# Places copied by GpSimd, scatters handed over together, an early base for the sums and separate weight loads in a routed expert layer

## The chip, the core and the metric

The kernel runs on one core of one Trainium2 chip. The metric is device time in microseconds of one execution; less is better. Instructions are issued in order on each engine: TensorE (PE, with its weight loads PEld), VectorE (DVE), ScalarE (ACT), GpSimd (POOL), and SyncE (SP), which here issues nearly all plain transfers. GpSimd issues the indirect ones.

## The reference

32 sequences of 256 tokens with 128 features: 8192 tokens. A modulation is computed for each sequence, then a gated linear recurrence along the tokens, then a mixture of 8 experts of which each token takes the best two.

```python
mod = (silu(c) @ wmod).reshape(32, 6, 1, -1)          # sa, ca, ga, sb, cb, gb
h = layernorm(x) * (1 + ca) + sa
g, a, v = sigmoid(h @ Wg.T + bg), sigmoid(h @ Wd.T + bd), h @ Wv.T + bv
x = x + ga * (scan(h_t = a_t * h_(t-1) + (1 - a_t) * v_t) * g)
h = layernorm(x) * (1 + cb) + sb
probs = softmax(h @ gate_w.T + gate_b)                # 8 experts, the top 2 are kept
y_e = relu(h @ w1[e] + b1[e]) @ w2[e] + b2[e]
x = x + gb * sum over the top 2 of probs_e * y_e
```

Before this, ga and gb are held at an absolute value of at least 0.25, with their sign.

## The kernel before

The 8192 tokens are cut into 16 supertiles of 512 tokens (s = 0 to 15; ST = 512, T = 4 groups of 128). Each goes through four steps, one step behind the other: a_norm (layer norm), a_mix (the recurrence), a_res (adding it to x, second layer norm) and a_route. HEAD and the loop over `steps` write the order of these steps by hand.

a_route picks two experts for each token, counts how many rows each expert has had so far (the product pq, L439 and L441, and the sum rk, L449), and so gets for each of the 2 x 512 rows a place in the DRAM array `reg`, in which each expert's rows lie together. The rows (`rw`: 128 features, the gate, the row's own number) are scattered to their places by eight indirect transfers of 128 rows each (L473), with the places read from the tile `pi`. They aren't issued at once: `sending` keeps them, and `drip` hands over one or two per step, each behind an ACT instruction that it names (`a["last"]`, `b["last"]`).

After some supertiles (TAKE, and the last one) `table` finds which full blocks of 256 rows the experts now have. There are 71 blocks. They enter `blocks` when drip has handed over the last scatter of that supertile (`held`). b_step moves a pipeline of blocks on by one:

- b_load: SP reads the block's expert and first row from the table (L561, L562), then loads the rows `xr` (L564, after the last sixteen reg scatters) and the expert's up weights `ww` (L570), four blocks ahead (LOOK).
- b_in: TensorE transposes the rows (L577) into `pbx`; ACT and DVE split them into two parts `xs` (L579, L580).
- b_up: twelve products (L592 to L594) into `p1`; ACT and DVE apply bias and relu (L598, L600).
- b_down: sixteen products (L611) into the one buffer `pby`; ACT scales by the gate into `yt` (L615, eight buffers); two indirect transfers (L617) scatter the 256 rows to the DRAM array `yd`, with the places read from `xr`.

`between` calls b_step between the steps of the supertiles while enough blocks wait. What is left runs alone at the end. When all blocks that hold rows of a supertile have gone through b_down, c_load loads its rows from yd (`yk`, L634) and transposes its gates (`pg`, L626, DVE L628), and c_add sums: yk's two halves (L648), the bias product pz (L644, added in L649), times the modulation gt (L642, L652), plus x (L653), and the result goes out (L654). The last supertile's sum waits for the last block.

The build runs with a scheduler: it takes each engine's order from its own simulation and the priorities in `high_priority`, so the order of the text is not the order of the queues.

## Time and profile before

| What | Value |
| --- | --- |
| Three runs, median (lowest to highest) | 541.54 us (541.11 to 545.75) |
| The profiled execution, its time | 542.55 us |
| The profiled execution, its span | 540.9 us |
| Mean granted TensorE clock | 0.861 |
| Moved by DMA | 91.57 MB, 169 GB/s over the span |
| Scatters to reg (L473) and to yd (L617) | 128 and 142 |
| GpSimd's time for one of them | 0.98 and 0.995 us |

The span reaches from the first to the last instruction. Busy shares are averages over stages with different limits: up to about 108 us the first supertiles are prepared and weights are staged, up to 342 us supertiles are routed with blocks between, then blocks run, and from 456 us blocks and sums. A line of the waits names the engine that waited, the line, and what came last before it went on; "issue" is time in which it waited for nothing that the profile shows. Landing is when a transfer's semaphore says that its data are there.

### The profile page before, as it was taken

To read this page: it belongs to the slowest core of one execution; us is meant where nothing else is said; L and a number is where in the kernel's file an instruction comes from. 1 tells how busy PE (TensorE), PEld (TensorE's weight loads), DVE (VectorE), ACT (ScalarE), POOL (GpSimd) and SP (SyncE) were. 2 spreads that over 40 slices of the span, in tenths; PEclk is the share of its full clock that TensorE was granted. 3 is DMA by queue.
4 is the path that set the end of the run, shared out by engine and by line. 5 is a ranking of instruction groups with operands and counts; after the bars stand their busy time and mean duration, and the time that the engine had idled before them with its cause. 6 is when DMAs were issued, how large, how long until landed. Compare 5 with 4: busy or idle time off the path is not lost. (4 is left out here: it accounts for less than half of the span.)

```text
span 540.9 us, 11312 instructions
## 1 busy us (share of the span) xinstructions
PE 419.9 (78%) x2771; PEld 361.6 (67%) x2771; DVE 305.4 (56%) x1607; ACT 288.2 (53%) x726; POOL 291.7 (54%) x322
## 2 busy tenths in 40 slices
PE   4668667696797878978698678778767999899971
PEld 3234424485676867758587577777666999899870
DVE  7999889583685756557367552412111220666565
ACT  4858355664757557467474453434243556566620
POOL 4535654445555666666565656556665355355531
PEclk9965666797879868997989897898989999899976
DMA  7993110754263534444351564457616887999853
GB/s 225 364 288 140 41 40 22 216 183 118 68 187 98 169 105 136 133 141 135 106 160 52 147 188 140 124 176 201 181 42 194 266 236 218 313 332 324 270 179 116
DMA packets 55414, 91.57 MB, mean 169 GB/s; under 512 B 8655, under 2 KB 39965, under 8 KB 55351
## 3 DMA queue, kind: packets, MB, share of 16 engines
q1 hardware_dynamic: 46624, 73.89, 45.6%
q0 software_dynamic: 8672, 16.94, 9.2%
q8 instruction: 25, 0.41, 0.3%
q14 instruction: 39, 0.31, 0.2%
q10 hardware_dynamic: 54, 0.02, 0.0%
HBM read 64.30 MB, written 27.43 MB: 170 GB/s over the span
## 5 line engine op out<-in xcount | busy, mean ns | idle before, releaser
L617 POOL DMA_INDIRECT yd<-yt,xr x142 | 141.3, 995 | 113.2 <-ACT yt L615 79.4
L611 PE MATMUL pby<-wr,hh 128*128 x1136 | 161.4, 298 | 26.5 <-ACT yt L615 21.3
L473 POOL DMA_INDIRECT reg<-rw,pi x128 | 125.5, 980 | 98.6 <-issue 43.5
L611 PEld LDWEIGHTS pby<-wr,hh 128*128 128x128 f32 x1136 | 152.1, 212 | 37.0 <-ACT yt L615 25.6
L600 ACT ACTIVATE hh<-p,ww 128x256 f32<-128x256 f32 x231 | 95.5, 481 | 46.0 <-remote 13.8
L615 ACT ACTIVATE yt<-pby,xr 128x128 f32<-128x128 f32 x142 | 44.6, 365 | 107.4 <-PE pby L611 30.5
L592 PE MATMUL p<-xs,ww 128*128 128x256 f32 x284 | 90.9, 321 | 12.9 <-DVE hh L598 6.3
L593 PE MATMUL p<-xs,ww 128*128 128x256 f32 x284 | 85.3, 300 | 0.1
L594 PE MATMUL p<-xs,ww 128*128 128x256 f32 x284 | 84.4, 297 | 0.5 <-issue 0.5
L580 DVE TENSOR_TENSOR xs<-pbx,xs 128x256 fp32r<-128x256 f32 x71 | 29.9, 420 | 83.6 <-ACT xs L579 38.1
L362 PE MATMUL pz<-h,wT 128*128 128x512 f32 x96 | 60.1, 750 | 11.0 <-DVE ta L374 7.4
L592 PEld LDWEIGHTS p<-xs,ww 128*128 128x128 f32 x284 | 57.7, 204 | 16.1 <-DVE hh L598 7.8
L594 PEld LDWEIGHTS p<-xs,ww 128*128 128x128 f32 x284 | 58.1, 204 | 1.1 <-issue 1.1
L593 PEld LDWEIGHTS p<-xs,ww 128*128 128x128 f32 x284 | 58.3, 205 | 0.7 <-issue 0.5
L598 DVE TENSOR_SCALAR hh<-p,ww 128x256 f32<-128x256 f32 x53 | 25.4, 479 | 28.8 <-ACT hh L600 20.8
L362 PEld LDWEIGHTS pz<-h,wT 128*128 128x128 f32 x96 | 20.8, 246 | 27.9 <-issue 17.1
L579 ACT ACTIVATE xs<-pbx 128x256 fp32r<-128x256 f32 x71 | 27.4, 386 | 14.1 <-PE pbx L577 6.6
L577 PE MATMUL pbx<-ident,xr 128*128 128x128 f32 x142 | 29.7, 289 | 5.2 <-DMA xr<-reg 2.8
L340 ACT ACTIVATE xn<-xa,nra,nya 128x128 f32<-128x128 f32 x64 | 26.5, 493 | 11.4 <-DVE nra L323 11.4
L398 ACT ACTIVATE xm<-xa,nrb,nyb 128x128 f32<-128x128 f32 x64 | 26.3, 485 | 9.6 <-DVE nrb L323 5.9
L648 DVE TENSOR_TENSOR ot<-yk 128x512 f32<-128x512 f32 (+1 forms) x17 | 11.2, 659 | 29.2 <-DMA yk<-yd 14.3
L577 PEld LDWEIGHTS pbx<-ident,xr 128*128 128x128 f32 x142 | 18.6, 150 | 7.5 <-issue 3.5
(188 smaller groups left out, 614.4 us busy)
## 6 DMA issues: line engine op xcount, KB each, us to landing
ww<-wd SPq DMA_DIRECT2D x71, 514.0 KB
xr<-reg SPq DMA_DIRECT2D x71, 130.0 KB
yk<-yd SPq DMA_DIRECT2D x30, 256.0 KB
wd<-wh SPq DMA_DIRECT2D x8, 514.0 KB
xa<-in_L_attn_x_dram SPq DMA_DIRECT2D x16, 256.0 KB
out_dram<-ot SPq DMA_DIRECT2D x15, 256.0 KB
yd<-yt,xr POOLq DMA_INDIRECT x142
w1s<-in_L_ffn_w_dram SPq DMA_DIRECT2D x8, 256.0 KB
```

Source lines behind the costliest of these rows:

```text
L362: nc.tensor.matmul(z, wT[:, i], h1, start=True, stop=True)
L473: w = nc.gpsimd.indirect_dma_start(out=reg, out_offset=bass.IndirectOffsetOnAxis(ap=pi[:, j * K + k:j * K + k + 1], axis=0), in_=rw[:, j, ...
L577: nc.tensor.transpose(px[:, j * P:(j + 1) * P], xr[:, j, 0:D], ident)
L579: nc.scalar.activation(xs[:, 0], px, AF.Copy)
L580: nc.vector.tensor_tensor(xs[:, 1], px, xs[:, 0], op=ALU.subtract)
L592: nc.tensor.matmul(z, hi, xs[:, 0], start=True, stop=False)
L593: nc.tensor.matmul(z, hi, xs[:, 1], start=False, stop=False)
L594: nc.tensor.matmul(z, lo, xs[:, 0], start=False, stop=True)
L600: w = nc.scalar.activation(hh[:, k], p1[:, k - k0], AF.Relu, bias=bias)
L611: nc.tensor.matmul(py[:, j * D:(j + 1) * D], hh[:, k, j * P:(j + 1) * P], we[:, k * D:(k + 1) * D], start=(j == 0 and k == 0), stop=(j == ...
L615: nc.scalar.activation(yt[:, j], py[:, j * D:(j + 1) * D], AF.Copy, scale=xr[:, j, D:D + 1])
L617: w = nc.gpsimd.indirect_dma_start(out=yd, out_offset=bass.IndirectOffsetOnAxis(ap=xr[:, j, D + 1:D + 2].bitcast(I32), axis=0), in_=yt[:, ...
```

## The change

- `place` copies the 128 places of one scatter into a small tile of its own (eight buffers in rotation), on GpSimd, in front of each scatter to reg and to yd. The scatter reads the copy.
- drip, sending and their waits are taken out. a_route issues its eight scatters itself. A table's blocks enter `blocks` at the next supertile's route step (those of the last table at once). Each block remembers how many scatters had been issued when its table was made, and its rows wait for the sixteen before that.
- b_load is parted: b_weights (four blocks ahead, LOOKW) and b_rows (three ahead, LOOKR), in this order in each step.
- c_base is new: from step CB0 = 28 on, and as soon as a supertile is counted, it computes the bias product, multiplies it by the modulation and adds it to x in place. c_add then sums yk's halves, multiplies and adds x. The modulation is spread twice, once for each (`spread`, `scaled`).
- From block 53 (HA) odd blocks take `pbx` and `pby` from the buffers that the routing used.
- yk has three buffers instead of two, ot three, which the constant b2f now shares; dgT has two instead of four.

```diff
...
+LOOKW = 4
+LOOKR = 3
 HA = 53
+CB0 = 28
...
     def late_constants():
-        b2f = cp.tile([P, T, D], F32, name="b2f")
+        b2f = wk.tile([P, T, D], F32, tag="ot", name="b2f", bufs=3)
         nc.gpsimd.memset(b2f, 0.0)
...
     nc.vector.tensor_copy(pad[:, :, D + 1].bitcast(I32), padi)
+    def place(column, name):
+        t = bk.tile([P, 1], I32, tag="place", name=name, bufs=8)
+        nc.gpsimd.tensor_copy(t, column)
+        return t
...
             w = nc.gpsimd.indirect_dma_start(
-                out=reg, out_offset=bass.IndirectOffsetOnAxis(ap=pi[:, j * K + k:j * K + k + 1], axis=0),
+                out=reg, out_offset=bass.IndirectOffsetOnAxis(ap=place(pi[:, j * K + k:j * K + k + 1], f"pp{s}_{j}{k}"), axis=0),
                 in_=rw[:, j, k], in_offset=None)
             into_reg(w.ins, "scat")
             return w.ins
-        sending.extend((s, send, j, k) for j in range(T) for k in range(K))
+        sent.extend(send(j, k) for j in range(T) for k in range(K))
         return rk[:, T]
-    sending = []
     sent = []
     held = []
-    def drip(n, behind):
-        for _ in range(min(n, len(sending))):
-            s, send, j, k = sending.pop(0)
-            w = send(j, k)
-            tc.add_manual_dep(w, behind.ins.name, WAIT, reason="pace of the rows on their way out")
-            sent.append(w)
-            if not sending or sending[0][0] != s:
-                while held and held[0][0] <= s:
-                    blocks.extend(held.pop(0)[1])
...
-    def b_load(n, tb, i):
+    def b_weights(n, tb, i):
         with tc.issue_after(loaded[-1].ins) if loaded else nullcontext():
             e = nc.sync.value_load(tb[i:i + 1, 0:1], min_val=0, max_val=E - 1)
+        ww = bk.tile([P, WW], F32, tag="ww", name=f"ww{n}", bufs=5)
+        loaded.append(nc.sync.dma_start(ww, wd[bass.ds(e, 1)].rearrange("o p f -> p (o f)")))
+        return dict(n=n, ww=ww, tb=tb, i=i)
+    def b_rows(b):
+        n, tb, i = b["n"], b["tb"], b["i"]
+        with tc.issue_after(loaded[-1].ins):
             r = nc.sync.value_load(tb[i:i + 1, 1:2], min_val=0, max_val=E * CAP)
         xr = bk.tile([P, NJ, RW], F32, tag="xr", name=f"xr{n}", bufs=YTB + 6)
         w = nc.sync.dma_start(xr, reg[bass.ds(r, BLK)].rearrange("(p t) d -> p t d", p=P))
         tc.add_to_no_dep_group("rows", w.ins)
-        for x in sent[-2 * K * T:]:
+        for x in b["sent"]:
             tc.add_manual_dep(w.ins, x.name, WAIT, reason="its rows")
-        ww = bk.tile([P, WW], F32, tag="ww", name=f"ww{n}", bufs=5)
-        b = dict(n=n, xr=xr, ww=ww, tb=tb, i=i)
-        loaded.append(nc.sync.dma_start(ww, wd[bass.ds(e, 1)].rearrange("o p f -> p (o f)")))
-        return b
+        loaded.append(w)
+        b["xr"] = xr
+    def own(n, tag, other):
+        if n >= HA and n % 2:
+            return psa.tile([P, 512], F32, tag=other, name=f"{tag}{n}")
+        return psb.tile([P, 512], F32, tag=tag, name=f"{tag}{n}")
     def b_in(b):
         n, xr = b["n"], b["xr"]
-        px = psb.tile([P, 512], F32, tag="pbx", name=f"pbx{n}")[:, :BLK]
+        px = own(n, "pbx", "pq")[:, :BLK]
         for j in range(NJ):
...
         n, xr, hh, i = b["n"], b["xr"], b["hh"], b["i"]
-        py = psb.tile([P, 512], F32, tag="pby", name=f"pby{n}")[:, :NJ * D]
+        py = own(n, "pby", "pt")[:, :NJ * D]
         e = nc.tensor.value_load(b["tb"][i:i + 1, 0:1], min_val=0, max_val=E - 1)
...
             w = nc.gpsimd.indirect_dma_start(
-                out=yd, out_offset=bass.IndirectOffsetOnAxis(ap=xr[:, j, D + 1:D + 2].bitcast(I32), axis=0),
+                out=yd, out_offset=bass.IndirectOffsetOnAxis(ap=place(xr[:, j, D + 1:D + 2].bitcast(I32), f"pd{n}_{j}"), axis=0),
                 in_=yt[:, j], in_offset=None, bounds_check=K * N - 1, oob_is_err=False)
             for g in ("yscat", "yrows"):
                 tc.declare_no_dep(w.ins, group=g, reason="rows of other pairs")
             tc.add_to_no_dep_group("yscat", w.ins)
+    def c_base(s):
+        pg = psa.tile([P, 512], F32, tag="pq", name=f"pg{s}")[:, :P + BPS * D]
+        nc.tensor.transpose(pg[:, :P], dgx[:, s].rearrange("p h t e -> p (h t e)").bitcast(F32), ident)
+        dgT = wk.tile([P, P], F32R, tag="dgT", name=f"dgT{s}")
+        nc.vector.tensor_copy(dgT, pg[:, :P])
+        g = spread(s, "pt")
+        pz = psa.tile([P, 512], F32, tag="pz", name=f"pb2{s}", bufs=2)
+        nc.tensor.matmul(pz, dgT, b2x.rearrange("p t d -> p (t d)"), start=True, stop=True)
+        t = wk.tile([P, T, D], F32, tag="ot", name=f"tb2{s}", bufs=3)
+        nc.scalar.activation(t.rearrange("p t d -> p (t d)"), pz, AF.Copy)
+        scaled(t, g, range(BPS))
+        nc.vector.tensor_tensor(xa[:, s], xa[:, s], t, op=ALU.add)
+    def spread(s, tag, bufs=1):
+        g = psa.tile([P, 512], F32, tag=tag, name=f"gt{tag}{s}", bufs=bufs)[:, :BPS * D].rearrange("p (q d) -> p q d", d=D)
+        for q in range(BPS):
+            b = s * BPS + q
+            nc.tensor.matmul(g[:, q], sel[:, b:b + 1].to_broadcast([N3, P]), mr3, start=True, stop=True)
+        return g
+    def scaled(t, g, qs):
+        for q in qs:
+            jq = slice(q * JB, (q + 1) * JB)
+            nc.vector.tensor_tensor(t[:, jq], t[:, jq], g[:, q].unsqueeze(1).to_broadcast([P, JB, D]), op=ALU.mult)
     def c_load(s):
-        pg = psa.tile([P, 512], F32, tag="pt", name=f"pg{s}")[:, :P]
-        nc.tensor.transpose(pg, dgx[:, s].rearrange("p h t e -> p (h t e)").bitcast(F32), ident)
-        dgT = wk.tile([P, P], F32R, tag="dgT", name=f"dgT{s}", bufs=4)
-        nc.vector.tensor_copy(dgT, pg)
-        yk = wk.tile([P, K, T, D], F32, tag="yk", name=f"yk{s}")
+        yk = wk.tile([P, K, T, D], F32, tag="yk", name=f"yk{s}", bufs=3)
         step = JB if s >= HALF else T
         for j0 in range(0, T, step):
             for k in range(K):
                 r = k * N + s * ST + j0 * P
                 w = nc.sync.dma_start(tiles(yk[:, k, j0:j0 + step]), tokens(yd, r, step * P))
                 tc.add_to_no_dep_group("yrows", w.ins)
-        return s, yk, step, dgT
-    def c_add(s, yk, step, dgT):
-        gt = psa.tile([P, 512], F32, tag="pq", name=f"gt{s}")[:, :BPS * D].rearrange("p (q d) -> p q d", d=D)
-        for q in range(BPS):
-            b = s * BPS + q
-            nc.tensor.matmul(gt[:, q], sel[:, b:b + 1].to_broadcast([N3, P]), mr3, start=True, stop=True)
-        pz = psa.tile([P, 512], F32, tag="pz", name=f"pb2{s}", bufs=2).rearrange("p (t d) -> p t d", d=D)
-        nc.tensor.matmul(pz, dgT, b2x, start=True, stop=True)
-        ot = wk.tile([P, T, D], F32, tag="ot", name=f"ot{s}")
+        return s, yk, step
+    def c_add(s, yk, step):
+        g = spread(s, "pz", 2)
+        ot = wk.tile([P, T, D], F32, tag="ot", name=f"ot{s}", bufs=3)
         for j0 in range(0, T, step):
             js = slice(j0, j0 + step)
             nc.vector.tensor_tensor(ot[:, js], yk[:, 0, js], yk[:, 1, js], op=ALU.add)
-            nc.vector.tensor_tensor(ot[:, js], ot[:, js], pz[:, js], op=ALU.add)
-            for q in range(j0 // JB, (j0 + step) // JB):
-                jq = slice(q * JB, (q + 1) * JB)
-                nc.vector.tensor_tensor(ot[:, jq], ot[:, jq], gt[:, q].unsqueeze(1).to_broadcast([P, JB, D]), op=ALU.mult)
+            scaled(ot, g, range(j0 // JB, (j0 + step) // JB))
             nc.vector.tensor_tensor(ot[:, js], ot[:, js], xa[:, s, js], op=ALU.add)
...
     nload = 0
-    LOOK = 4
+    based = 0
+    counted = []
+    nrows = 0
     def b_step():
-        nonlocal nload
+        nonlocal nload, nrows
+        nonlocal based
         i = len(flow)
-        while nload < len(blocks) and nload < i + 1 + LOOK:
-            tb, q, ends = blocks[nload]
-            blocks[nload] = b_load(nload, tb, q)
-            blocks[nload]["ends"] = ends
+        while nload < len(blocks) and nload < i + 1 + LOOKW:
+            tb, q, ends, n = blocks[nload]
+            blocks[nload] = b_weights(nload, tb, q)
+            blocks[nload].update(ends=ends, sent=sent[n - 2 * K * T:n])
             nload += 1
+        while nrows < nload and nrows < i + 1 + LOOKR:
+            b_rows(blocks[nrows])
+            nrows += 1
         b = blocks[i] if i < len(blocks) else None
         flow.append(b)
         if b:
             b_in(b)
         if i >= 1 and flow[i - 1]:
             b_up(flow[i - 1])
-            drip(1 if alive else 2, flow[i - 1]["last"])
         if i >= 2 and flow[i - 2]:
             b_down(flow[i - 2])
             ended.extend(flow[i - 2]["ends"])
+        if i >= CB0 and based < min(NS, len(counted)):
+            c_base(based)
+            based += 1
         if len(adding) >= CLAG or (adding and not ended and i >= len(blocks)):
...
                 base = a_route(st[s], base)
+                counted.append(s)
                 if s in CLS:
                     b = cp.tile([P, E], F32, name=f"cnt{s}")
                     nc.vector.tensor_copy(b, base)
                     base = b
                     counts.append(b)
-                nb = len(blocks) + sum(len(x) for _, x in held)
+                while held:
+                    blocks.extend(held.pop(0))
+                nb = len(blocks)
                 if s in TAKE:
                     n = full(s) - nb
                     tb, done = table(s, counts[:1] * (s > CUT) + [base], done, n, False)
-                    held.append((s, [(tb, q, []) for q in range(n)]))
+                    held.append([(tb, q, [], len(sent)) for q in range(n)])
                 elif s == NS - 1:
                     n = touched(s) - nb
                     tb, done = table(NS, counts, done, n, True)
                     fills(base)
-                    rest = [(tb, q, []) for q in range(n)]
-                    held.append((s, rest))
+                    rest = [(tb, q, [], len(sent)) for q in range(n)]
+                    blocks.extend(rest)
                     z = 0
...
             (step0, step1, step2, step3)[i](s)
-            drip(2 if t < len(steps) - NS or len(sending) > K * T else 1, st[s]["last"])
             between()
...
```

1 line of the change is left out of this document (removed).

## The prediction

> **What bounds the kernel now.** I read the page first, then the busy time by stage, then the same view for the down products of line 611 alone. These run sixteen to a block, so their count tells how many of the 71 blocks a stage finishes.
>
> The whole-page shares:
>
> ```profile
> PE 419.9 (78%) x2771; PEld 361.6 (67%) x2771; DVE 305.4 (56%) x1607; ACT 288.2 (53%) x726; POOL 291.7 (54%) x322
> PEclk9965666797879868997989897898989999899976
> DMA  7993110754263534444351564457616887999853
> ```
>
> TensorE is the busiest at 78%, but it is not full in every stage. The next three lines are line 611 alone, in three stages; the columns are the stretch in us, its length, PE busy and count, weight loads busy and count, clock, DMA share and GB/s.
>
> ```profile
> 108.00:337.50 229.50, 72.29 (x480) 68.01 (x481) 0.88 0.45 133
> 337.50:418.00 80.50, 34.57 (x240) 32.47 (x240) 0.90 0.52 151
> 418.00:456.00 38.00, 20.22 (x160) 18.94 (x160) 1.00 0.83 249
> ```
>
> 480, 240 and 160 matmuls are 30, 15 and 10 blocks: 7.65, 5.37 and 3.80 us for each. The first stage still routes supertiles. In the second no supertile is left to route (the last pq product of L439 runs at 341.9 us), yet the pace is far from what TensorE can do. What it can do stands in the chain of waits, where the down products start 3.43 to 3.45 us apart with nothing between but other matmuls:
>
> ```profile
> 440.42 1.78 PE pby L611 x16
> 443.87 1.79 PE pby L611 x16
> 447.30 1.86 PE pby L611 x16
> ```
>
> So the stretch from 337.5 to 418 is the slow zone: 15 blocks at 5.37 us where 3.43 would do. What fills it is GpSimd's queue. There the scatters of the last three supertiles are still handed over one or two per step, each behind an ACT instruction. The waits, in us, times and longest:
>
> ```profile
> POOL yd L617 <- ACT yt L615: 79.4, 46, 5.1
> POOL reg L473 <- ACT hh L600: 19.0, 9, 4.1
> POOL reg L473 <- ACT xm L398: 12.3, 6, 5.6
> SPq L564 <- DMA reg<-rw,pi: 60.6, 18, 11.6
> ```
>
> The last reg scatter starts at 406.5 us, 64.6 us after the last pq, and SP, which may not load the rows of the last table before it has landed, issues no load from 386.3 to 408.9. From 418 TensorE is full; from 456 the sums of the output join, at a DMA share of 0.92.
>
> **The change, part by part.** The sum is made against the profiled execution: 542.55 us, a span of 540.9 and 1.65 around it; the median of the three times, 541.54, lies 1.0 below it.
>
> *Handing over at once (the pace and its waits go).* In the order in which the changed kernel is built, the last pq on TensorE stands behind the down product of block 37; before it stands behind that of block 30. The last reg scatter on GpSimd stands behind the yd scatters of block 33, before behind those of 40. So eight blocks (30 to 37) move from the slow zone under the routing, and the 17 from 38 to 54 can run at the full pace. Before, the 25 blocks 30 to 54 take 456 - 337.5 = 118.5 us. After, 17 x 3.43 = 58.3 us, and the eight cost what they add to the routing stage. Bounds: 3.43 each (packed into TensorE's gaps: by the busy time by stage 229.5 us hold 185.2 of work) is 27 us, 7.65 each (that stage's own pace, routing included) is 61 us. I take 5.37, the pace they have now beside reg scatters: 43 us. Result so far: 118.5 - 58.3 - 43 = 17 us less (bounds 33 less, 1 more).
>
> *The bases.* All sixteen c_base stand before block 38's down product. TensorE: pg 0.27 (L626), pb 0.48 (L644), two gt of 0.225 (L642), 1.2 us x 16 = 19 us if all is on the path, 0 if it fits in the 44 us of gaps. DVE gets two products of 0.415 (L652) and a sum of 0.69 (L653) for each, 24 us, ACT a 512-wide copy (0.69, as L366), 11 us; DVE is busy 135 of 229.5 us there and hides them. If that cover were gone, 1.5 us a supertile would show. I take 6 us more.
>
> *The copies of places.* 270 copies join GpSimd's queue, 196 scatters of which come before the end of the reg scatters (128 and 68). A COPY of 128x4 takes 0.184 us (L264). One that stands between two scatters is seen here:
>
> ```profile
> 251.42 0.98 POOL L617 DMA_INDIRECT yd<-yt,xr  x1 [0.30 <-issue]
> 252.70 0.97 POOL L473 DMA_INDIRECT reg<-rw,pi  x1 [0.30 <-issue]
> 253.66 0.38 POOL L462 COPY rw<-dst 128x8 int32<-128x8 int32 x1
> 254.20 0.98 POOL L473 DMA_INDIRECT reg<-rw,pi  x1 [0.16 <-issue]
> ```
>
> The copy fills the 0.30 us between two scatters, so a pitch of 1.28 becomes 1.50. Bounds for one copy: 0.08 (the median 0.225 of L462 in that gap) and 0.385 (0.225 and a 0.16 gap of its own); I take 0.15, x 196 = 29 us. There are eight buffers, so each copy waits until the scatter eight back has landed, and the rest of the queue waits behind it: the scatters of the yt tiles, and through these ACT and TensorE once eight yt are full. By the built order, up to the end of the reg scatters 5 copies stand directly behind the scatter that they wait for and 25 with one scatter between; the rest have two or more. Landing, from issue, bounded by the two ends that the chain shows:
>
> ```profile
> 451.87 4.29 DMA yd<-yt,xr
> 529.67 2.23 DMA yd<-yt,xr
> ```
>
> Directly behind: 2.23 to 4.29 less one pitch of 1.28, x 5 = 5 to 15 us; one between: 0 to 1.73, x 25 = 0 to 43. I take 20 us, nearer the low end since the first of these two had four scatters in a row behind it. Against that the ACT waits of L473 go: 19.0 + 12.3 + 4.9 + 4.7 + 4.2 + 2.1 = 47 us. Net for GpSimd 29 + 20 - 47 = 2 us; since the eight now stand in one lump before yd scatters, I put 3 us on the path. After the reg scatters 14 copies stand directly behind and 15 one behind their scatter, in pairs. A pair then takes 1.28 + 2.23 + 0.22 + 0.16 = 3.9 us at least where the blocks come every 3.43, 0.5 x 14 = 7 us, which the eight yt buffers (8 x 3.43 = 27 us) cover; were they gone, 7 us would show, at 4.29 us 35.
>
> A rule speaks against the copies. The Trainium skill, SBUF — State Buffer, section Who interferes with whom, says that a GpSimd instruction that reads SBUF is blocked for the whole of a DVE instruction with two SBUF inputs. The trace has GpSimd copies from 0.198 to 0.414 us (L462), so 0.22 us of delay at most; by the rule a copy behind an L653 would lose 0.69 us, and 196 of them at worst 135 us, by the row at worst 43. I go by the row.
>
> *Weights apart.* A ww load no longer stands behind SP's wait for reg (60.6 us in 18 waits). Block 45's up product starts 9.3 us after its loads are issued, the blocks before have 5 to 10 us in hand, so only that one place gains: it is in the 17 us already. 0 more; if a weight came late, each block would show SP's two or three issues of 0.33 us. Rows are asked for three blocks ahead instead of four, 3 x 3.43 = 10 us, where 5 to 10 are needed; the third yk and ot buffers and the shared buffer of b2f cost no instruction.
>
> *The tail from 456.* Leaving it: pg and pb from TensorE (0.12 + 0.24 us apart as issued, 0.36 x 13 = 4.7 us), one DVE sum of 0.69 (L649) of each of the sums. TensorE now waits for DVE ahead of pb (us, times):
>
> ```profile
>   DVE ot L649: 13.8, 11
> ```
>
> With 6.8 ahead of gt that is 20.6 us. This wait stays in part: gt moves to pz's two buffers and still waits for the product of the sum two back, which needs that sum's yk. The second pby and pbx for odd blocks from 53 help only where TensorE isn't already full. The DMA share of 0.92 leaves 0.08 x 57 = 4.6 us in this stage and more after 513. I take 6 us less (bounds 0 and 15).
>
> *Sum.* 542.55 - 17 + 6 + 3 - 6 = 528.5 profiled, 527.5 against the median; I say 527. The bounds add up to 497 and 566, the two outer rivals.
>
> **The rivals.** *GpSimd's queue becomes the bound (slower).* Place: 108 to 418 us, reg scatters, copies and yd scatters in one queue. There it holds 196 x 1.28 = 251 us of 310, so 59 are free. At the high ends the copies add 75 and the waits 58 us, less the 47 of removed pace: 86 us, 27 over what is free; it decides from 59 us on. Lumps of eight also hold up yd, which I price by the longest single wait of SP for reg, 11.6. Together 39 us: 527 + 39 = 566, and from 14 us over the 59, slower than now. For it: queue already 81% taken. Against it: the built order leaves two or more scatters between for 166 of the 196 copies.
>
> *The gain is given back (within 1%).* The eight blocks cost 7.65 each (61 us, 1 more instead of 17 less) and DMA bounds the tail: 541.5 + 1 + 6 + 3 - 6 = 545.5, or 539.5 if the bases fit in the gaps. For it: the routing stage has that pace today.
>
> *All is packed.* Eight blocks at 3.43, bases hidden, tail 15: 541.5 - 33 - 15 + 3 = 497. Against it: no routing stage so far has run TensorE above 81%.
>
> *The change doesn't do it:* if the first reg scatters of each supertile still waited for ACT through the rw buffers (three), the slow zone would stay; that is 541.
>
> **How the numbers follow.** Forecast 0.5 (its own range 515 to 536), packed 0.12, given back or without effect 0.14, GpSimd bound 0.24. About 1%, 5.4 us, is what a measurement can tell from no change. Faster: 0.5 and 0.12, 0.62 in all; within 1%: 0.12; slower: 0.26, which is the GpSimd case and a bit of the second. The range goes to 503 below (half way into the packed case) and 556 above (most of the GpSimd case).
>
> **What would show it.** Right: line 611 counts 38 blocks by about 390 us, then 3.43 to 3.6 us a block until the first sum; no reg scatter after that; SP's wait for reg much below 60.6 us. Wrong: GpSimd near 90% busy with COPY waiting for DMA, yt waiting for yd; line 611 above 4 us a block after the last pq; the last down product later than now (524.6 us).

## The result, and the profile after

The changed kernel takes 607.75 us (median of four, 605.51 to 611.65), the kernel before 542.75 (four, 541.11 to 545.75): ratio 1.122, 95% interval 1.116 to 1.128. It was forecast faster, at 527 us, and is slower by 65. The profiled execution has a span of 604.9 us.

From the page, two lines that answer to those shown of before. GpSimd (POOL) is busy for 48.8 us more, which is less than the time lost, and no engine is near full:

```profile
PE 432.2 (71%) x2803; PEld 365.4 (60%) x2803; DVE 321.4 (53%) x1638; ACT 300.8 (50%) x742; POOL 340.5 (56%) x592
DMA  8972250225443524535354250414557771399983
```

The DMA row dips to 1 near the end (`771399`), where the last ten slices of before hold nothing under 3. Line 621 (before: 611) alone, the down products, sixteen to a block; columns as in the prediction:

```profile
128.00:353.50 225.50, 69.69 (x480) 65.29 (x480) 0.89 0.43 127
353.50:413.00 59.50, 18.32 (x128) 16.93 (x128) 0.83 0.28 83
413.00:466.00 53.00, 17.08 (x112) 15.23 (x112) 0.77 0.57 170
466.00:527.00 61.00, 22.18 (x176) 21.00 (x176) 0.82 0.47 143
```

30 blocks at 7.5 us, 8 at 7.4, 7 at 7.6, then 11 in 61 us. Read by the start of a block's first down product:

| block | before, us | changed, us | later by |
|---|---|---|---|
| 0 | 109.5 | 129.4 | 20 |
| 30 | 337.7 | 353.7 | 16 |
| 38 | 383.6 | 418.0 | 34 |
| 45 | 420.8 | 466.9 | 46 |
| 55 | 457.6 | 499.7 | 42 |
| 56 | 466.0 | 527.8 | 62 |
| 70 | 524.6 | 589.3 | 65 |

So three places lose: the start (20 us), the end of the routing between blocks 30 and 45 (30 us more), and the step from block 55 to 56, which takes 28.1 us instead of 8.4.

**The start and the end of the routing.** GpSimd's instructions in order of time, with the idle time ahead of each and what ended it:

```profile
103.10 0.59 POOL L289 COPY pp<-pi 128x1 int32<-128x1 int32 x4 [19.97 <-DVE pi L467]
...
112.99 0.96 POOL L484 DMA_INDIRECT reg<-rw,pp  x1 [0.30 <-issue]
...
394.79 1.01 POOL L289 COPY pp<-pi 128x1 int32<-128x1 int32 x8 [9.82 <-DVE pi L467]
...
406.83 0.99 POOL L627 DMA_INDIRECT yd<-yt,pd  x1 [0.17 <-issue]
```

In both places the next supertile's copies stand first in GpSimd's queue and wait for places that DVE has not computed yet, 20 us at the start and 9.8 at 385. What stands behind them is late: block 0's rows, which SP may load when the scatter issued at 112.99 has landed (at 115.3; before 96.8), and at 406.8 the yd scatter of block 33, whose yt was ready at 371.7.

The scatter of 112.99 is the 32nd to reg. By the kernel's text (`sent[n - 16:n]`, five blocks from the first table) block 0's rows need no scatter behind the 24th, issued at 81.95. But SP's wait for them, from 86.0 on, ends with the landing of the 32nd, and so it does in all seven traces of kernels that hand over at once. Why the wait reaches that far isn't shown. The start's loss goes with handing over at once, not with the copies: of the runs below, block 0 starts at 131.3 and 132.4 us in the two that hand over at once without copies where the kernel before takes 540 to 545 us, and at 109.3 and 111.6 in the two that have the copies and the pace of before.

The waits, GpSimd's first and then SP's (us, times, longest):

```profile
POOL pp L289 <- DVE pi L467: 43.1, 5, 20.0
POOL pd L289 <- DMA yd<-yt,pd: 32.9, 25, 3.1
POOL yd L627 <- ACT yt L625: 31.6, 15, 7.1
```

```profile
SPq L570 <- DMA reg<-rw,pp: 83.4, 6, 29.2
SPq L666 <- DMA yd<-yt,pd: 31.5, 4, 26.3
```

The 79.4 us for which GpSimd waited for ACT's yt have shrunk to 31.6; a wait for DVE's pi of 43.1 and one for landed scatters have come in their place. SP's wait for reg has grown from 60.6 to 83.4.

**The step to block 56.** GpSimd in the tail:

```profile
503.13 0.98 POOL L627 DMA_INDIRECT yd<-yt,pd  x1 [0.30 <-issue]
504.18 0.18 POOL L289 COPY pd<-xr 128x1 int32<-128x1 int32 x1
505.43 0.18 POOL L289 COPY pd<-xr 128x1 int32<-128x1 int32 x1 [1.07 <-DMA yd<-yt,pd]
506.21 0.99 POOL L627 DMA_INDIRECT yd<-yt,pd  x1 [0.60 <-POOL pd L289]
507.51 0.97 POOL L627 DMA_INDIRECT yd<-yt,pd  x1 [0.30 <-issue]
```

A copy waits 1.07 us for a landed scatter, the scatter behind it starts 0.60 us after the copy's end, and a pair comes every 507.51 - 503.13 = 4.38 us, where TensorE delivers a block every 3.3 (blocks 45 to 55 of the table); at blocks 41 to 47 the pairs are 5 to 9 us apart. The yd scatters fall behind, from 1.8 us after their yt at block 40 to 29 us at block 55. The first sum's yk load in SP's queue waits 26.3 us for them, and behind it stand the rows of block 58 (493.5 for block 57, 524.6 for 58):

```profile
493.52 0.34 SPq L570 DMA_DIRECT2D xr<-reg  x1
496.12 0.34 SPq L562 DMA_DIRECT2D ww<-wd  x1
522.85 0.90 SPq L666 DMA_DIRECT2D yk<-yd  x2
524.57 0.36 SPq L570 DMA_DIRECT2D xr<-reg  x1
```

TensorE transposes the rows of block 58 ahead of the down product of block 56 and has nothing to do until they come:

```profile
501.79 1.28 PE L621 MATMUL pby<-wr,hh 128*128 x10
527.39 0.66 PE L587 MATMUL pbx<-ident,xr 128*128 128x128 f32 x2 [24.33 <-DMA xr<-reg]
```

The Trainium skill, DMA: Bandwidth & Descriptors, section Anatomy of one DMA — SWDGE (gpsimd) path, gives such a DMA a fixed 2.0 us or so, most of it the wait until the write is confirmed; the chain of waits shows 2.24 to 2.28 us for these scatters, which agrees.

### The profile page after: what moved, and what is told of

Its sections match the earlier page's. It is cut to its first block, busy times and chain, and to the rows that moved or that the text cites. A ratio compares the mean times of both kernels' runs of the same rounds, so it can differ in the third digit from the quotient of the medians.

```text
span 604.9 us, 11679 instructions
## 1 busy us (share of the span) xinstructions
PE 432.2 (71%) x2803; PEld 365.4 (60%) x2803; DVE 321.4 (53%) x1638; ACT 300.8 (50%) x742; POOL 340.5 (56%) x592
## 4 chain that ended last, share of the span: by engine, by line
PE 49%; issue 12%; DVE 10%; another core or an unknown queue 8%; POOL 7%; DMA 7%; ACT 5%; SPq 1%; POOLq 0%; ACTq 0%; DVEq 0%
PE pby L621 21%; PE p L602 5%; PE p L604 5%; POOL reg L484 5%; PE p L603 5%; PE pz L373 3%; PE pbx L587 2%; PE pl L424 2%; DMA yd<-yt,pd 1%; DMA ww<-wd 1%; ACT hh L610 1%; ACT xm L409 1%; DMA wr<-in_L_ffn_w_dram 1%; DMA xr<-reg 1%
## 5 line engine op out<-in xcount | busy, mean ns | idle before, releaser
L627 POOL DMA_INDIRECT yd<-yt,pd x142 | 141.8, 999 | 100.6 <-ACT yt L625 31.6
L621 PEld LDWEIGHTS pby<-wr,hh 128*128 128x128 f32 x1136 | 149.3, 206 | 32.7 <-issue 14.9
L484 POOL DMA_INDIRECT reg<-rw,pp x128 | 125.4, 979 | 31.2 <-issue 24.7
L610 ACT ACTIVATE hh<-p,ww 128x256 f32<-128x256 f32 x231 | 97.4, 477 | 73.2 <-PE p L604 20.1
L373 PE MATMUL pz<-h,wT 128*128 128x512 f32 x96 | 62.7, 773 | 22.1 <-ACT aa L379 8.3
L602 PEld LDWEIGHTS p<-xs,ww 128*128 128x128 f32 x284 | 58.1, 208 | 13.1 <-issue 7.2
L603 PEld LDWEIGHTS p<-xs,ww 128*128 128x128 f32 x284 | 59.2, 209 | 3.5 <-issue 3.0
L604 PEld LDWEIGHTS p<-xs,ww 128*128 128x128 f32 x284 | 58.8, 207 | 1.5 <-issue 1.5
L289 POOL COPY pp<-pi 128x1 int32<-128x1 int32 x128 | 23.9, 217 | 56.3 <-DVE pi L467 43.1
L289 POOL COPY pd<-xr 128x1 int32<-128x1 int32 x142 | 26.6, 212 | 39.2 <-DMA yd<-yt,pd 32.9
```

The lines of the kernel that those rows point to most:

```text
L289: nc.gpsimd.tensor_copy(t, column)
L373: nc.tensor.matmul(z, wT[:, i], h1, start=True, stop=True)
L484: w = nc.gpsimd.indirect_dma_start(out=reg, out_offset=bass.IndirectOffsetOnAxis(ap=place(pi[:, j * K + k:j * K + k + 1], f"pp{s}_{j}{k}") ...
L602: nc.tensor.matmul(z, hi, xs[:, 0], start=True, stop=False)
L603: nc.tensor.matmul(z, hi, xs[:, 1], start=False, stop=False)
L604: nc.tensor.matmul(z, lo, xs[:, 0], start=False, stop=True)
```

## The experiments

Runs of one group share a chip and its runs of the kernel before, and the groups fell on four chips (the last two on one): the kernel before takes 540 to 545 us in the first two and 471 to 472 us in the other three. Ratios are against before on the same chip, with a 95% interval.

**First group (before: 545.5 us).** Theory A: handing over at once costs in the routing, the copies in the tail. B: the copies alone. C: the early bases.

The changed kernel without copies:

```diff
...
-ap=place(pi[:, j * K + k:j * K + k + 1], f"pp{s}_{j}{k}")
+ap=pi[:, j * K + k:j * K + k + 1]
...
-ap=place(xr[:, j, D + 1:D + 2].bitcast(I32), f"pd{n}_{j}")
+ap=xr[:, j, D + 1:D + 2].bitcast(I32)
```

> The changed kernel without GpSimd's copies: every scatter reads its places from the tile that holds them, as before; all else as changed. Theory A (two losses: in the routing stage the eight scatters at once, from 57 to 46 us of delay by block 45; in the tail the copies, whose pairs go out every 4.35 us where the blocks come every 3.43): the tail's part goes, about 20 to 28 us of the 65, and the routing stage keeps its delay: 580 us (570 to 590). Theory B (the copies alone: their waits for landed scatters sum to 47 us in the waits of the changed kernel, and they hold the queue): nearly all comes back, 545 us (540 to 555). Theory C (the early bases hold TensorE and the banks from block 25 on): at most the tail comes back, 585 us or more.

Measured: 616.1 us, 1.131 (1.124 to 1.139). All three were wrong on the sum. The step from block 55 to 56 falls to 4 us, as A said of the tail, but block 45 starts at 490 us, 23 later than with copies. Nothing now stands between the scatters: they go out in runs of eight to sixteen, and waits without a visible releaser ("remote") grow, DVE's for line 403 to 51.1 us from 7.0.

The changed kernel with the sums as before: c_base goes, c_load and c_add are those of the kernel before, with two yk buffers.

```diff
...
-        if i >= CB0 and based < min(NS, len(counted)):
-            c_base(based)
-            based += 1
```

> The changed kernel with the sums as they were before (no early base; two yk buffers instead of three, since the old form needs the room). Theory C (the sixteen early bases stand where the loss begins, from the eleventh supertile's routing on): 40 to 50 us come back, 560 us. Theories A and B: the bases cost at most their 1.2 us of TensorE each where the routing stage is late anyway, and the sums get back what they gained: 600 to 612 us.

Measured: 607.5 us, 1.113 (1.106 to 1.120): C falls. The last pq product does come 54 us earlier (356 against 410), but the last reg scatter only 13 us (410 against 423) and the end not at all.

The pace of before put back, copies and bases kept:

```diff
...
+            tc.add_manual_dep(w, behind.ins.name, WAIT, reason="pace of the rows on their way out")
...
+            drip(1 if alive else 2, flow[i - 1]["last"])
...
+            drip(2 if t < len(steps) - NS or len(sending) > K * T else 1, st[s]["last"])
```

> The changed kernel with the pace of before (scatters of a supertile handed over one or two per step, each behind an ACT instruction, blocks released when the last of them is issued); copies, early base and separate weights stay. Theory A: the routing stage's delay goes (35 to 46 us by block 45), the tail's stays (20 to 28): 565 us (558 to 578). Theory B: the copies stay and so does the loss: 595 to 610 us. Theory C: 600 us.

Measured: 588.4 us, 1.076 (1.068 to 1.085), between A and B.

The kernel before with copies alone:

```diff
...
+ap=place(pi[:, j * K + k:j * K + k + 1], f"pp{s}_{j}{k}")
...
+ap=place(xr[:, j, D + 1:D + 2].bitcast(I32), f"pd{n}_{j}")
```

> The kernel before, with GpSimd's copies added and nothing else changed. Theory A: the routing stage is paced as before and loses little (196 copies by at most 0.15 us, partly hidden), the tail's pairs go out every 4.35 instead of 3.43 to 3.96 us: 565 us (555 to 575). Theory B: 595 to 610 us. Theory C: no change beyond 1%: 540 to 548 us.

Measured: 576.2 us, 1.058 (1.052 to 1.065). The copies cost 31 us by themselves: block 45 is 15 us late, block 56 29. So they are not all of it.

**Second group (before: 539.7 us).** Diffs against the changed kernel; the first has the pace and no copies.

> The changed kernel with the pace of before and without copies; early base, separate weights and the other buffers stay. Three costs are now supposed: the copies (31 us where the pace of before stands: 576 against 545), the handing over at once, and the early bases (with them the twelfth pq product comes 57 us after the eleventh, without them 22 to 26). Theory D, all three cost: 588 less the copies' 31 is 557 us (550 to 565), and what is left above the kernel before, 12 us, is the bases'. Theory E, the bases only fill gaps: 541 to 548 us.

Measured: 547.9 us, 1.012 (1.004 to 1.021). Without the bases too, which leaves the weights apart, the third ot buffer and the second banks:

> The kernel before with the separate weights, the third sum buffer and the second banks of the odd late blocks alone: pace of before, no copies, sums as before. Prediction: weights apart cost and gain nothing in the middle, the second banks at most some us in the tail: 541 to 546 us. If SP's order were one of the costs: above 550 us.

Measured: 546.0 us, 1.010 (1.002 to 1.019). The weights apart cost at most 1%. The bases with the sums that they shorten come to nothing that can be told (1.9 us), but this is the balance of two effects: with them block 54 starts 11.5 us later (461.9 against 450.4), and from there to block 70 it takes 68.5 us instead of 76.4. Now that kernel with the eight handed over at once:

```diff
...
-        sending.extend((s, send, j, k) for j in range(T) for k in range(K))
+        sent.extend(send(j, k) for j in range(T) for k in range(K))
...
```

> The run before this one with the eight scatters of a supertile handed over at once; no copies, sums as before. Theory D: the run of ten to sixteen scatters back to back holds TensorE's completions (in the changed kernel without copies, lags up to 10 us after such runs), once in each of thirteen supertiles, 4 to 5 us each: 590 to 605 us. Theory E, that handing over at once frees the queue as predicted and only copies and bases cost: 525 to 541 us.

Measured: 594.0 us, 1.100 (1.090 to 1.110). Handing over at once costs 48 us by itself on this chip (594.0 against 546.0), as D said. By blocks, against the kernel of 546.0: block 0 starts 27 us later (131.3 against 104.3), the first thirty blocks take 36 us more (264.7 against 228.2), and the 25 behind them 21 us less (104.7 against 125.8). Last, the first of these four with a later base:

```diff
-CB0 = 28
+CB0 = 42
```

> As the first run of these four, with the first early base fourteen steps later, behind the routing of most supertiles (step 42 instead of 28). Theory D: the bases no longer stand before the routing of the last four supertiles and cost nothing there, and the tail has less to do for each sum: 538 us (530 to 545). Theory E: the same as the first run of these, within 1%.

Measured: 541.1 us, 1.003 (0.998 to 1.007), no difference from before, and 6.8 us less than with bases from step 28.

The changed kernel, the first group and this one make a table, all on chips where before takes 540 to 545 us (* without the weights apart):

| | no copies | copies |
|---|---|---|
| pace, sums as before | 1.010 | 1.058* |
| pace, bases | 1.012 | 1.076 |
| at once, sums as before | 1.100 | 1.113 |
| at once, bases | 1.131 | 1.122 |

The costs don't add up. The copies cost 5 to 6% with the pace and 1% either way without it; handing over costs 9 to 12% without copies, 5% with them; the bases cost between nothing and 3%. The rows come from different chips, so 1% between them says nothing.

How completions come late is seen in the timeline of the kernel that hands over at once alone: GpSimd's run of ten scatters, TensorE's down product, ACT's next instruction.

```profile
247.42 0.96 POOL L484 DMA_INDIRECT reg<-rw,pi  x1 [0.78 <-issue]
...
258.98 0.98 POOL L627 DMA_INDIRECT yd<-yt,xr  x1 [0.30 <-issue]
```

```profile
250.24 1.95 PE L621 MATMUL pby<-wr,hh 128*128 x16
```

```profile
261.75 0.62 ACT L625 ACTIVATE yt<-pby,xr 128x128 f32<-128x128 f32 x2 [8.73 <-remote]
```

The product is done at 252.2, ACT is idle from 253.0, and yt starts at 261.75, 1.8 us after the run of scatters has ended (259.96). "remote" is what the profile writes where nothing that ended then explains the wait; we read it, with one core, as a completion that became known late. The semaphore that ACT waits for here is TensorE's: TensorE ends six instructions that raise it between 252.2 and 260.1 us, but one event is recorded at 254.53 and the next six between 261.73 and 262.02.

Over the whole trace, the time from a matmul's modelled end to the next recorded event of that semaphore is 0.014 us at the median outside runs of scatters, and 1.8 us from 3 us into a run of three or more (gaps under 0.5 us) to its last scatter. It is 1.9 in the changed kernel without copies, 1.5 in the changed kernel and 2.0 in before. In these traces 11 to 14% of the events have no record (here 429 of 484 have one), which lengthens the figure, so it gives the size and no more. ACT's events lag too (1.3 in this run). Before has these waits as well, from the runs of four to nine that the pace lets through:

```profile
ACT yt L615 <- remote: 20.3, 5, 6.1
```

**Third group (before: 472.2 us).** A chain of TensorE and ACT, then of DVE and ACT, by itself, to measure this lag; behind the last sum of the kernel before:

```diff
...
+nc.tensor.transpose(pv[:, :P], ca_[:, :P], ident)
+last = nc.scalar.activation(ca_[:, :P], pv[:, :P], AF.Copy)
...
```

> The kernel before, and behind its last sum a chain measured by itself: a TensorE transpose of 128x128, an ACT copy of the result, the next transpose, and so on, one link after another; beside it first nothing on GpSimd, then sixteen scatters back to back, then eight pairs of scatters each behind the fourth link after the last pair, then twenty-four GpSimd memsets of 128x512; after that the same with a DVE copy in TensorE's place. The added part writes only rows that nothing reads any more. Theory F (a run of scatters holds back the completions of the other engines): a link takes under 1.5 us beside nothing, beside pairs and beside memsets, and 2 to 10 us from the third scatter of a run on, 20 us of run holding fewer than half of the links that 20 us of nothing hold. Theory G (in the changed kernel the waits come from what stands behind what, and a run by itself holds nothing): links within 20% of each other in all parts.

Measured: every link of the first chain 0.84 us, in all parts, of the second 0.60 to 0.67. Theory F failed here. The chain beside the run of sixteen:

```profile
511.50 0.28 ACT L789 ACTIVATE ca__8882<-pv 128x128 f32<-128x128 f32 x1 [0.56 <-PE pv L788]
511.63 0.96 POOL L799 DMA_INDIRECT reg<-pad,pidx  x1 [0.30 <-issue]
512.34 0.28 ACT L789 ACTIVATE ca__8882<-pv 128x128 f32<-128x128 f32 x1 [0.56 <-PE pv L788]
```

But on this chip the kernel before itself is some 70 us faster than in the groups ahead, and no completion is late in any run of it: 0.014 us at the median inside runs too.

The kernel with the weights apart (546.0 us above), with the order that the pace makes but without its wait (ORDER raises no semaphore):

```diff
...
-            tc.add_manual_dep(w, behind.ins.name, WAIT, reason="pace of the rows on their way out")
+            tc.add_manual_dep(w, behind.ins.name, ORDER, reason="pace of the rows on their way out")
```

> As the sixth run (weights apart, no copies, sums as before), with the scatters in the queue spread as the pace of before spreads them, but without their waits for ACT: the edge that sets the order stays, the semaphore wait goes (runs of reg scatters in the queue up to six long, most one to three). Theory F (long runs cost, the pace pays by breaking them): 540 to 552 us, near the 546 with waits. Theory G (the wait itself is what helps, since it lets yd scatters and the routing go first): nearer the 594 of handing over at once, 565 or more.

Measured: 466.7 us, 0.989 (0.985 to 0.993).

The kernel before with copies and 32 place buffers:

```diff
...
-        t = bk.tile([P, 1], I32, tag="place", name=name, bufs=8)
+        t = bk.tile([P, 1], I32, tag="place", name=name, bufs=32)
```

> The kernel before with GpSimd's copies, which cost 31 us with eight place buffers, and 32 buffers for the places instead of eight: the copies stay, their waits for landed scatters go. If the waits are the cost: 541 to 550 us. If the copies' own time in the queue is (270 of 0.2 us and the pause behind each): 560 to 576 us.

Measured: 497.1 us, 1.053 (1.050 to 1.056), 25 us more than before. Waits for landed scatters fall to 4.6 us in all, but here GpSimd's queue is full: scatters and copies back to back from 327 to 375 us, the last reg scatter at 362 us against 336 in the run above, block 45 after that. So the copies cost where the queue is the bound, by their own time and by waits for their rows (18.7 us in 13 places for xr); the two weren't separated.

**Fourth group (before: 472.0 us).** The same questions once more, first the changed kernel itself.

> The changed kernel, once more, on whichever chip this call gets, beside the chain measured by itself (next run). Theory F (runs of scatters hold back completions, on chips that do so): where the kernel before takes about 540 us, ratio 1.11 to 1.13 as before; where it takes about 472 us, the routing stage's loss is gone and only the copies' queue time and tail are left: ratio 0.99 to 1.05. Theory G (what stands behind what in the queues costs, whatever the chip): 1.10 or more on either.

Measured: 537.4 us, 1.145 (1.128 to 1.162). So the changed kernel loses 65 us here too, where no completion is late (0.014 us): the late completions aren't needed for its loss. By blocks against the order without wait on this chip: block 0 112 against 97 us, block 30 304 against 274, 45 400 against 345, 56 461 against 386. The chain again, then the last two again:

> The chain of TensorE and ACT, then of DVE and ACT, beside nothing, a run of sixteen scatters, pairs, and memsets, as in the ninth run, where every link of the first chain took 0.84 us, beside the scatters too. Theory F: where the kernel before takes about 540 us, links beside the run of sixteen stretch to 2 to 10 us from the third scatter on, and stay below 1.5 us beside memsets; where it takes about 472 us, 0.84 us again. Theory G: 0.84 us on either, and what makes the 540 is not the scatters.

Measured: 0.84 us a link once more, with DVE in TensorE's place 0.60, beside scatters up to 0.66.

> The scatters spread in the queue as by the pace, without the wait for ACT; no copies, sums as before. Where the kernel before takes about 540 us, Theory F: 540 to 552 us if spreading alone is what helps, ratio 1.00 to 1.02; if the wait itself is needed, ratio 1.04 to 1.08, since without it runs of four to six scatters come back to back more often. Where it takes about 472 us: ratio 0.985 to 0.995 again.

Measured: 466.8 us, 0.994 (0.988 to 0.999).

> The kernel before with copies and 32 place buffers. In the eleventh run it cost 5.3% where GpSimd's queue was full from scatter to scatter, against 5.8% with eight buffers where the kernel before takes 545 us. Where the kernel before takes about 540 us GpSimd waits for ACT more than 79 us, so the copies' own time is hidden there, and without their waits for landed scatters the ratio is 1.00 to 1.02; if it is the copies' time that costs there too, 1.04 to 1.06.

Measured: 494.5 us, 1.055 (1.042 to 1.068). Neither was run where the kernel before takes 540 us.

**Fifth group (before: 471.2 us).** Handing over at once alone, the kernel of 594.0 us, where no completion is late:

> Handing over at once alone (no copies, sums as before), as the seventh run. Theory F (its 48 us came from completions held back by runs of scatters): where the kernel before takes about 472 us, none of that: 455 to 475 us, ratio 0.97 to 1.01, and the 17 us that were forecast show at least in part; where it takes about 540 us, ratio 1.09 to 1.11 again. Theory G (the eight block the queue while their places are not known, whatever the chip): ratio 1.05 or more on either.

Measured: 460.4 us, 0.975 (0.968 to 0.982): faster by 11 us, weights apart included. The chain's shares by engine, of the same program on the second group's chip and on this one:

```profile
PE 49%; another core or an unknown queue 16%; issue 10%; DVE 9%; ACT 7%; DMA 6%; SPq 2%; POOL 1%; POOLq 0%; ACTq 0%; DVEq 0%
```

```profile
PE 56%; DMA 18%; DVE 8%; ACT 5%; POOL 4%; issue 4%; SPq 3%; POOLq 0%; ACTq 0%; DVEq 0%
```

16% of 583.4 us, 93 us on the chain that we read as late completions, against none. And the down products alone in the first 38 blocks, second group's chip, then this one:

```profile
131.00:396.00 265.00, 72.10 (x481) 67.76 (x482) 0.83 0.38 113
396.00:437.00 41.00, 18.26 (x128) 16.64 (x128) 0.88 0.59 178
```

```profile
112.00:267.00 155.00, 60.24 (x480) 57.47 (x479) 1.00 0.61 180
267.00:316.00 49.00, 18.52 (x128) 17.11 (x129) 0.86 0.60 181
```

The first thirty blocks take 265 us or 155; blocks 38 to 54 take 63 or 62, and from block 55 to the start of block 70 it is 67 or 65. The two runs differ in the start (block 0 at 131 or 112) and in the stage in which eight scatters at once stand beside the routing, and hardly anywhere else. Late completions aren't the whole difference of that stage: TensorE is busy 192 us of the 265 and 154 of the 155, at a granted clock of 0.83 and 1.00, so some 38 of the 110 us are the same work done more slowly (matmul ends are modelled) and 72 are waiting. Why the clock differs isn't shown.

Where the 11 us come from is seen against the kernel before in the chain run of the fourth group, on the same chip: block 0 starts 7 us later (112 against 104), the first thirty blocks take 23 us less (155 against 178), and the 25 behind them 4 us more (110 against 107, from 110.3 and 106.8). So on this chip the gain stands under the routing and not, as forecast, behind it.

The changed kernel with places of its own for each supertile and block:

```diff
...
-        t = bk.tile([P, 1], I32, tag="place", name=name, bufs=8)
...
+            n, b = (T * K, 2) if head[1] == "p" else (NJ, 6)
+            places[head] = bk.tile([P, n], I32, tag=head[:2], name=head, bufs=b)
+        t = places[head][:, c:c + 1]
```

> The changed kernel with the places in tiles of their own, one of eight columns for a supertile (two of them) and one of two columns for a block (six), so that no copy waits for one of the two scatters right ahead of it; the copies themselves stay, as many and as long. If the tail's loss is the waits for landed scatters: the pairs go out with the blocks, the jump of 27 us ahead of block 56 is gone, and the time falls by 20 to 30 us: ratio 1.07 to 1.10 instead of 1.12 to 1.145. If it is the copies' time: no change, 1.12 or more.

Measured: 500.1 us, 1.058 (1.050 to 1.066), 37 us less than the changed kernel on this chip and more than the 20 to 30 expected. GpSimd's waits for landed scatters at the copies fall from 48 us to 1.1. Blocks 55 and 56 start at 421 and 424 us, where they were at 433 and 461: the tail's loss was these waits. Others have come in their place, ahead of copies that now stand further forward in the queue:

```profile
POOL pd L295 <- DMA xr<-reg: 27.1, 14, 3.8
```

The version that the runs point to, the spread order without wait, no copies, bases from step 42:

> Scatters spread as by the pace but without the wait, no copies, weights apart, and the early bases from step 42 on, after the routing of most supertiles. Spreading without waits gave 0.989 and 0.994 where the kernel before takes 472 us, and the later base 0.75% (541 against 546): ratio 0.98 to 0.99 there. Where it takes 540 us: 0.99 to 1.01.

Measured: 464.5 us, 0.983 (0.976 to 0.990), faster than both kernels where the kernel before takes 471 us, though there handing over at once alone was faster still (460.4); where before takes 540 neither this version was tried nor the spread order without wait.

## Why the prediction was wrong, point by point

- **Handing over at once, 17 us less.** On the chip where it costs 48 us, the step did what its two terms said: the eight blocks were put at 43 us and take 41, the seventeen at 58.3 and take 63, and the 25 together take 21 us less than with the pace. What failed is what the sum left out. It held the start and the first thirty blocks at their time; they take 27 and 36 us more. Part of the start is lost on either kind of chip (block 0 at 112 instead of 97 us against the spread order in the fourth group), with SP's wait for the 32nd scatter ahead of it. The thirty blocks depend on the chip: where completions are late beside runs of scatters, runs of ten and twelve scatters, reg and yd together, stand where the pace lets through four to nine. That these runs are the cause is argued from the waits and from the same program's two times; how they hold completions back isn't shown. Where no completion is late the step gains 11 us, but in the first thirty blocks, which the prediction held fixed; the 25 blocks from which it took its 17 us take 110 us, no less than the 107 of before there. So the right sign on that chip is luck. The prediction read "remote" waits of before as nothing in particular; 20.3 us of them stood at yt alone.
- **The copies, 3 us more.** This is the step that fails on both kinds of chip. Alone they cost 31 us with the pace of before (576 against 545 us), and within the changed kernel places of their own give back 37 us (537 against 500) where no completion is late. The term was mis-sized in two places. The tail was put at 3.9 us a pair for 14 pairs, 7 us, "which the eight yt buffers" cover; it measures 5 to 9 us a pair for seven blocks and 4.38 from there, since the copies with one scatter between wait as well and 0.60 us, not 0.16, lie between such a copy and its scatter. From 440 to 527 us the waits hold 26.6 us in 21 places, and the yd scatters end 29 us behind. And the cover fails where the prediction did not look: not at yt, but at the first sum's yk load, which waits 26.3 us in SP's queue with block 58's rows behind it. The pace waits of 47 us that were set against all this do go, but 47.4 us of waits for landed scatters (32.9 + 6.3 + 5.4 + 2.8), where 20 were put, and 43.1 of waits for pi replace them; those for pi belong to handing over at once, as the start shows. The copies with 32 buffers cost 23 and 25 us where the queue is full, near the 29 put for their own time, but part of that is waits for rows.
- **The rule weighed.** A copy took 0.21 us in the mean, as put. Single copies do show the rule of the Trainium skill (SBUF — State Buffer, Who interferes with whom): GpSimd beside DVE's sum of two SBUF inputs,

```profile
415.64 0.70 POOL L289 COPY pp<-pi 128x1 int32<-128x1 int32 x1
```

```profile
415.62 0.68 DVE L646 TENSOR_TENSOR xa<-xa,tb 128x512 f32<-128x512 f32 x1
```

  the copy lasts until DVE is done, 0.70 instead of 0.18 us. It happens to few: the 78 copies that overlap a DVE instruction of 0.3 us or more take 0.272 us in the mean (median 0.196), the 192 others 0.191, which makes 6 us over all of them. The row was the right side for the sum.
- **The bases, 6 us more, and the tail, 6 us less.** The runs show the two together, put at 0: 1.9 us with the pace (547.9 against 546.0) and none in the changed kernel (607.75 against 607.5, in different groups). Apart, by blocks of the first pair: 11.5 us more up to block 54, since the bases hold up the routing (the pq product of supertile 12 comes at 296 us instead of 275), and 8 us less from there. Both terms had their sign. In the changed kernel the tail's gain is covered: from block 56 to 70 it takes 61.5 us, before 58.6. Handed over at once without copies, the bases seem to cost more, 1.131 against 1.100 on two chips.
- **Weights apart, 0.** 1% at most, on the slow side.
- **The rivals.** "GpSimd's queue becomes the bound" had the right side and the right place for half of it, at 566. It looked for a full queue, 90% busy; the queue stands at 56%, and its waits bound. The sign "the last down product later than now" came: 589.3.

What the parts make on the chip of the fourth and fifth group: handing over at once -11, copies without waits for landed scatters 23, those waits 37, together 49 of the 65 us. The other 16 lie in what the kernels of 460.4 and 500.1 us still differ by, copies that wait for rows (27.1 us of such waits) and the bases; they were not separated. Where completions are late, the parts alone (48 and 31 us) exceed the whole of 65. A likely reason, not tested by itself, is that copies break up the runs of scatters (the lag is 1.5 us with them, 1.9 without).

## What to carry to other kernels

A queue that serves two streams in order must not be handed work whose inputs aren't there yet: count for each added instruction what it waits for and who stands behind it, in the next queue as well (here GpSimd's pairs, then SP's sums, then TensorE's rows). A wait that recurs with every block is priced by the pitch that it makes against the pitch that feeds it, over all blocks, not by the buffers that hide the first few. And a pacing that looks like idle time may be what keeps another cost small: take it out alone before building on the room.

## What the runs showed of the hardware that was not expected

- The same program on different chips: 594.0 and 460.4 us (handing over at once alone), 540 to 545 and 471 to 472 (before), 607.75 and 537.4 (changed). A verdict may turn with it: 1.100 against 0.975.
- On the slower of these, completions of TensorE and ACT become known late while GpSimd issues scatters back to back, TensorE's by 1.5 to 2.0 us at the median from 3 us into a run (with 11 to 14% of the events unrecorded), and ACT idle for 8.7 us in the place shown; from 3 us after a run on, the median is 0.014 us again. On the faster, neither the kernels nor a chain beside sixteen scatters (0.84 us a link) show it.
- What makes the two differ, the chip or something beside it at the time, is open, and so is how the scatters hold completions back: the chain by itself was never on a chip that does so.
